# Folding the last query columns of a head with their rotation partners into one tile, and transposing the probabilities two quarters behind their scores

## The chip, the cores and the metric

The kernel runs on one core of one Trainium2 chip. The metric is the device time of one execution in microseconds (us). Engines are named as in the profile: PE is TensorE, PEld its weight loads, DVE is VectorE, ACT is ScalarE, POOL is GpSimd, SP is SyncE.

## The reference, cut to what matters

Four residual steps act on x of 4 x 512 x 512 (batch, sequence, width). In front of each stands a layer norm. The first is a sparse mix along the sequence: for each row of a 512 x 512 similarity the 153 largest entries are kept. The second is a feed-forward layer with a Hadamard rotation and weights quantized to three values, the fourth another one without the rotation. The change lies in the third, a latent attention with 16 heads:

```python
q_hk = (hidden_q @ Wq.T).reshape(Bv, Sv, H, K)
q_big = jnp.einsum('bshk,hkq->bshq', q_hk, w_kc_q)          # 384 query columns per head
q_big = _apply_rope(q_big, sin_q[None, :, None, :], cos_q[None, :, None, :])
q_r = jnp.einsum('bshq,hqr->bhsr', q_big, W_qr)             # 64 columns per head
k_r = jnp.einsum('bld,hdr->bhlr', kv_r, W_kr)
attn = jax.nn.softmax(jnp.einsum('bhsr,bhlr->bhsl', q_r, k_r), axis=-1)
ctx_c = jnp.einsum('bhsl,bld->bhsd', attn, kv_r)
```

`_apply_rope` multiplies each of the 384 columns by its cosine and adds its partner times the sine; the partner of column c is c + 192 or c - 192, with the sign in the sine table.

## The kernel before, in words

Everything of the attention is held transposed, query columns on partitions and the 512 positions along the free dimension, in f32. The loop in `attention` (L798) runs over 32 pairs of heads: 4 batches times 8 groups `g`. While the scores of the current pair are worked on, the queries of the next pair are prepared, in four quarters `j` of 128 positions. A quarter writes `cur.scores(j)`, then a piece of the next pair (`head`, `rope`), then `cur.turn(j - 1)`, the transposes of the quarter before. After the fourth quarter come `nxt.rotated()`, `cur.turn(3)`, `cur.attended()` and `cur.added()`.

- `head(i)` (L674) makes the 128 latent query values `qh` of head i of the pair with four matmuls (L677).
- `rope(i)` (L685) multiplies `qh` by two blocks of `wc` into two PSUM tiles `pb` and rotates them. For i = 0 and 1 these are the first 128 columns of a head and their partners (columns 0 to 127 and 192 to 319, `_query_chunks` L964), with full 128-column matmuls (L693). What is left of a head is 64 columns and 64 partners. In step i = 2 one tile holds the last 64 columns of both heads, the other the partners of both, each written by two 64-column matmuls with `halves` (L661 to L665). VectorE multiplies each tile by the cosine into `ro` (L707) and the other tile by the sine into `rs` (L708); POOL adds the two (L709). `ro` has 7 buffers, `rs` 3.
- `rotated` (L712) multiplies the six `ro` by `wr` into one tile `pr`, the upper 64 rows for one head and the lower 64 for the other: twice `halves` for the first four `ro` (L663, L665), then two full 128-column matmuls (L726) for the last two `ro`, whose block of `wr` has zeros off the diagonal because both heads lie in one tile. ScalarE copies `pr` to `qr` (L731).
- `scores(j)` (L736) has one matmul for each head with 64 rows (L744, L747), VectorE's maximum `nm` (L752), ScalarE's exponential (L755), VectorE's reciprocal (L757) and ScalarE's scaling (L758) of the probabilities `pp`, which have 5 buffers.
- `turn(j)` (L761) transposes the two `pp` of a quarter on TensorE (L766) and copies them to `pT` (L767). `attended` (L769) multiplies `pT` with `kv` into `pc` (L774); `added` (L782) makes `po` (L786) and adds it to x (L791).

The matmul outputs `pqh`, `pb`, `pr`, `pss`, `pc` and `po` share one ring of 4 PSUM tiles. Between the quarters, pieces of background work are written: the top-k search of the next batch (L403, L405) and the feed-forward layers of other batches, each with a planned cost and a due time (L891 to L916). They don't depend on the attention of the same batch. The framework then lays down a fixed order of instructions for each engine, from the order in which they are written, their priorities (`tc.high_priority` for the second of two half-sized matmuls) and its own costs; on the chip each engine runs its order and waits at semaphores. The tags `pp` and `ro` also serve the first and the last stage, when no attention runs (`front_t` L86, `gate_t` L91).

Of the kernel before, what the change touches and what calls it, by code (L numbers as in the profile page):

```python
# [9 lines left out]
F32 = mybir.dt.float32  # L10
# [23 lines left out]
def flamingo_kernel(  # L34
# [51 lines left out]
    def front_t(name):  # L86
        if mine("front", 2):
            return two_k("front", 3, name)
        return wp.tile([P, 512], F32, tag="pp", name=name, bufs=5)
# [30 lines left out]
    cos_q = const.tile([P, 4, S], F32, tag="cosq", name="cos_q")  # L120
    sin_q = const.tile([P, 4, S], F32, tag="sinq", name="sin_q")
# [504 lines left out]
    def hidden_T(b):  # L626
        mv, r = ln_stats([xs[b, j] for j in range(NT)], f"q{b}")
        t = hp.tile([P, NC, S], F32, tag="hT", name=f"hT_{b}", bufs=1)
        for j in range(NT):
            n = wp.tile([P, D], F32, tag="pp", name=f"nq_{b}_{j}", bufs=5)  # L630
# [7 lines left out]
    def query_weights(b, g):  # L638
# [9 lines left out]
        wr = hp.tile([P, 4 * P], F32, tag="wr", name=f"wr_{u}", bufs=1)  # L648
# [18 lines left out]
    class Pair:  # L667
# [17 lines left out]
        def rope(self, i):  # L685
# [3 lines left out]
            for o in range(2):  # L689
                pb = mm_ps(f"pb_{self.u}_{i}_{o}")  # L690
                if i < 2:
                    at = (2 * i + o) * P
                    nc.tensor.matmul(  # L693
                        pb, self.wc[:, at : at + P], self.qhs[i], start=True, stop=True
                    )
                else:
                    at = (4 + o) * P
                    halves(
                        pb, (self.wc[:, at : at + 64], self.wc[:, at + 64 : at + P]), self.qhs,
                        start=True, stop=True,  # L700
                    )
                both.append(pb)
            for o in range(2):
                t = 2 * (i // 2) + o
# [3 lines left out]
                nc.vector.tensor_tensor(rs, both[1 - o], sin_q[:, t, :], ALU.mult)  # L708
# [3 lines left out]
        def rotated(self):  # L712
# [5 lines left out]
            for o in range(2):  # L718
                halves(
                    pr,  # L720
                    (wr[:, 64 * o : 64 * o + 64], wr[:, P + 64 * o : P + 64 * o + 64]),
                    (ros[o], ros[2 + o]),
                    start=(o == 0), stop=False,
                )
            for o in range(2):
                nc.tensor.matmul(  # L726
                    pr, wr[:, (2 + o) * P : (3 + o) * P], ros[4 + o],
                    start=False, stop=(o == 1), skip_group_check=True,
                )
# [6 lines left out]
        def scores(self, j):  # L736
# [12 lines left out]
            for i in range(2):  # L749
# [3 lines left out]
                pp = wp.tile([P, S], F32, tag="pp", name=f"pp_{v}", bufs=5)  # L753
# [44 lines left out]
    def attention(first):  # L798
# [4 lines left out]
        for at, (b, g) in enumerate(order):  # L803
# [3 lines left out]
            for j in range(NT):  # L807
# [13 lines left out]
                if j:  # L821
                    cur.turn(j - 1)
                yield b, g
            if nxt:
                nxt.rotated()
            cur.turn(NT - 1)
# [120 lines left out]
def _constants():  # L947
# [6 lines left out]
    a, a1, c, c1 = _query_chunks()  # L954
# [91 lines left out]
```

## Time and profile before

| What | Time or value |
|---|---|
| median of 3 runs | 2158.28 us (2158.27 to 2160.31) |
| the profiled execution | 2156.5 us |
| its span, first to last instruction | 2154.7 us |
| mean granted TensorE clock | 0.952 |
| 0 to 300 us: first batch's top-k search and feed-forward layer | PE busy 173.3 us, DVE 231.7 us |
| 310 to 1985 us: the 32 pairs | PE idle 96.1 us in all |
| 1985 to 2155 us: the last feed-forward layer | PE busy 140.8 us, DVE 109.5 us |

The page gives busy time for each engine over the whole span, then the span in 40 slices of 53.9 us, each digit a tenth of busy time. A line of the timeline is: start in us, duration in us, engine, line of the code, operation, output from input, the shape of the stationary part for a matmul (rows * columns), output shape from input shape, count; in brackets idle time of the engine in front of it and what ended that. One f32 matmul in the code is two records in the trace. Matmul ends are modelled and overlap the next start, so the distance between starts is the cost.

### The profile page before, as it was taken

What the parts mean: (1) busy time and instruction counts of PE and PEld (TensorE: products, weight loads), DVE (VectorE), ACT (ScalarE), POOL (GpSimd) and SP (SyncE); (2) the same over time, 40 slices, a digit from 0 to 9 for tenths busy, and PEclk for the clock granted to TensorE, in tenths of its full rate; (3) what the DMA queues carried; (4) which work ended last, traced back from release to release, by engine and by line L of the source; (5) the groups of instructions that cost most, each with busy time, mean ns of one, the idle gap of its engine ahead of it and who ended that gap; (6) DMA issues with size and microseconds to landing.
All of it is one profiled execution on the core that took longest, in us unless ns stands there. A gap on an engine that the chain in (4) does not pass through costs nothing.

```text
span 2154.7 us, 21904 instructions
## 1 busy us (share of the span) xinstructions
PE 1901.2 (88%) x7402; PEld 889.7 (41%) x7402; DVE 1571.2 (73%) x3124; ACT 1216.3 (56%) x1991; POOL 347.6 (16%) x332
## 2 busy tenths in 40 slices
PE   1259789999999999899989998999889899999978
PEld 0125534444444434444443334445444344444433
DVE  7986679986676999666669997656637445756765
ACT  6836445445554553466445544565697765567534
POOL 3032012123100121310111222101111110101000
PEclk6579999999999999999999999999999999999989
DMA  7452101111110211111112111111566211111000
GB/s 271 149 182 87 45 27 54 42 47 33 37 32 15 86 49 42 37 37 31 32 28 86 47 44 42 28 29 33 171 217 214 62 37 48 60 37 35 15 15 20
DMA packets 62176, 140.30 MB, mean 65 GB/s; under 512 B 7152, under 2 KB 10608, under 8 KB 58736
## 3 DMA queue, kind: packets, MB, share of 16 engines
q1 hardware_dynamic: 56592, 122.44, 17.9%
q0 software_dynamic: 4320, 14.16, 1.8%
q10 hardware_dynamic: 1152, 2.30, 0.3%
q8 instruction: 59, 0.97, 0.2%
q14 instruction: 53, 0.43, 0.1%
HBM read 118.95 MB, written 19.92 MB: 64 GB/s over the span
## 4 chain that ended last, share of the span: by engine, by line
PE 50%; DVE 34%; ACT 10%; issue 3%; POOL 2%; DMA 1%; SPq 0%; DVEq 0%; POOLq 0%; ACTq 0%
DVE work L405 8%; PE pc L774 7%; DVE m L403 7%; PE po L786 7%; PE pqh L677 5%; DVE nm L752 4%; PE pzh_f L502 3%; PE pss L744 2%; DVE rs L708 2%; PE pu_g L291 2%; PE pd_g L363 2%; PE pd_f L363 2%; PE pg_g L291 2%; PE pu_f L291 2%; PE pb L693 2%
## 5 line engine op out<-in xcount | busy, mean ns | idle before, releaser
L709 POOL TENSOR_TENSOR ro<-ro,rs 128x512 f32<-128x512 f32 x192 | 253.9, 1326 | 1415.8 <-DVE rs L708 1203.1
L755 ACT ACTIVATE pp<-pss,nm 128x512 f32<-128x512 f32 x256 | 175.1, 687 | 257.2 <-DVE nm L752 256.3
L774 PE MATMUL pc<-pT,kv 128*128 128x512 f32 x512 | 244.2, 605 | 14.5 <-ACT pT L767 14.4
L677 PE MATMUL pqh<-hT,wq 128*128 128x512 f32 x512 | 238.6, 606 | 5.0 <-ACT pp L755 3.0
L786 PE MATMUL po<-om,cxo 128*128 128x512 f32 x512 | 231.3, 597 | 1.1 <-ACT cxo L779 1.1
L752 DVE TENSOR_REDUCE nm<-pss 128x1 f32<-128x512 f32 x256 | 169.1, 680 | 78.9 <-PE pss L747 77.5
L403 DVE MAX8 m<-work 128x8 f32<-128x512 f32 x304 | 209.4, 689 | 5.0
L405 DVE MATCH_REPLACE8 work<-m,work 128x512 f32<-128x512 f32 x288 | 194.2, 674 | 0.0
L758 ACT ACTIVATE pp<-pp,rsm 128x512 f32<-128x512 f32 x256 | 179.1, 723 | 25.9 <-DVE rsm L757 25.6
L767 ACT COPY pT<-ppt 128x512 f32<-128x512 f32 x256 | 142.5, 590 | 69.6 <-PE ppt L766 69.6
L766 PEld LDWEIGHTS ppt<-ident,pp 128*128 128x128 f32 x1024 | 119.9, 143 | 95.3 <-issue 46.6
L791 DVE SCALAR_TENSOR_TENSOR x<-po,gt,x 128x512 f32<-128x512 f32 x128 | 95.3, 745 | 86.6 <-PE po L786 85.6
L766 PE MATMUL ppt<-ident,pp 128*128 128x128 f32 x1024 | 148.3, 280 | 10.0 <-ACT pp L758 8.8
L677 PEld LDWEIGHTS pqh<-hT,wq 128*128 128x128 f32 x512 | 93.6, 191 | 132.2 <-issue 93.5
L744 PE MATMUL pss<-kr,qr 64*128 64x512 f32 x256 | 143.4, 641 | 5.1 <-ACT pp L755 4.3
L747 PE MATMUL pss<-kr,qr 64*128 64x512 f32 x256 | 144.6, 645 | 3.4 <-DVE ro L707 3.0
L786 PEld LDWEIGHTS po<-om,cxo 128*128 128x128 f32 x512 | 93.8, 190 | 114.7 <-issue 96.3
L707 DVE TENSOR_TENSOR ro<-pb,cos_q 128x512 f32<-128x512 f32 x192 | 129.8, 676 | 11.1 <-PE pb L693 9.7
L708 DVE TENSOR_TENSOR rs<-pb,sin_q 128x512 f32<-128x512 f32 x192 | 130.1, 678 | 8.9 <-PE pb L693 5.7
L774 PEld LDWEIGHTS pc<-pT,kv 128*128 128x128 f32 x512 | 92.2, 192 | 99.9 <-issue 76.9
L693 PE MATMUL pb<-qh,wc 128*128 128x512 f32 x256 | 126.0, 609 | 6.5 <-ACT qh L682 6.5
L490 DVE TENSOR_TENSOR yb_f<-ya_f 128x1024 f32<-128x1024 f32 x64 | 77.0, 1230 | 15.0 <-PE ph_f L496 14.7
(256 smaller groups left out, 3220.6 us busy)
## 6 DMA issues: line engine op xcount, KB each, us to landing
wq<-in_wqh SPq DMA_DIRECT2D x64, 256.0 KB, 2.6
om<-omd SPq DMA_DIRECT2D x64, 256.0 KB, 2.7
wc<-in_wkcq SPq DMA_DIRECT2D x32, 384.0 KB, 3.0
wr<-in_wqr SPq DMA_DIRECT2D x32, 256.0 KB, 2.6
krd<-krs POOLq DMA_DIRECT2D x32, 256.0 KB, 2.3
kr<-krd SPq DMA_DIRECT2D x32, 256.0 KB, 2.6
sa_w1v<-in_gvT SPq DMA_DIRECT2D x8, 1024.0 KB, 5.3
sb_w1v<-in_gvT SPq DMA_DIRECT2D x8, 1024.0 KB, 6.7
```

Of the source, the lines that this page charges most:

```text
L403: nc.vector.max(m8, cur)
L405: nc.vector.match_replace(work, m8, cur, GONE)
L677: nc.tensor.matmul(pq, self.wqs[i][:, c, :], hT[self.b][:, c, :], start=(c == 0), stop=(c == NC - 1),)
L708: nc.vector.tensor_tensor(rs, both[1 - o], sin_q[:, t, :], ALU.mult)
L709: nc.gpsimd.tensor_tensor(ro, ro, rs, ALU.add)
L744: nc.tensor.matmul(*args, start=True, stop=True)
L752: nc.vector.tensor_reduce(nm, pss[i], AX.X, ALU.max, negate=True)
L755: nc.scalar.activation(pp, pss[i], AF.Exp, bias=nm, accum_out=sm)
L758: nc.scalar.activation(pp, pp, AF.Copy, scale=rs)
L766: nc.tensor.transpose(pt[:, l, :], pp[:, l * P : (l + 1) * P], ident)
L774: nc.tensor.matmul(pc, kv[self.b][:, l, :], self.pT[i][:, l, :], start=(l == 0), stop=(l == NT - 1),)
L786: nc.tensor.matmul(po, self.cxo[i][:, j * P : (j + 1) * P], self.oms[i], start=(i == 0), stop=(i == 1),)
```

## The change

The last step of `rope` is laid out by head instead of by kind. Tile o of step 2 now holds, for head o, its last 64 columns on partitions 0 to 63 and their 64 partners on partitions 64 to 127, made by one full matmul from `qhs[o]`. The cosine multiply is one operation as before. The sine multiply is written as two operations on 64 partitions each, since the partner now lies in the other half of the same tile: partitions 64 to 127 of `pb` go to 0 to 63 of `rs`, and the reverse. In `rotated` the last two `ro` are then multiplied like the others, with one more `halves`, and the zeros in `wr` are gone: `wr` is 192 KB a pair instead of 256, and the cosine and sine tables have 3 blocks of 512 columns instead of 4.

The transposes of a quarter are written two quarters after its scores instead of one: `turn(0)` in quarter 2, `turn(1)` in quarter 3, `turn(2)` and `turn(3)` after `nxt.rotated()`. `pp` has 7 buffers instead of 5, everywhere where the tag is used.

```diff
@@ rope
-                if i < 2:
-                    at = (2 * i + o) * P
-                    nc.tensor.matmul(
-                        pb, self.wc[:, at : at + P], self.qhs[i], start=True, stop=True
-                    )
-                else:
-                    at = (4 + o) * P
-                    halves(
-                        pb, (self.wc[:, at : at + 64], self.wc[:, at + 64 : at + P]), self.qhs,
-                        start=True, stop=True,
-                    )
+                at = (2 * i + o) * P
+                nc.tensor.matmul(
+                    pb, self.wc[:, at : at + P], self.qhs[i if i < 2 else o], start=True, stop=True
+                )
                 both.append(pb)
             for o in range(2):
-                t = 2 * (i // 2) + o
+                t = o if i < 2 else 2
...
                 nc.vector.tensor_tensor(ro, both[o], cos_q[:, t, :], ALU.mult)
-                nc.vector.tensor_tensor(rs, both[1 - o], sin_q[:, t, :], ALU.mult)
+                if i < 2:
+                    nc.vector.tensor_tensor(rs, both[1 - o], sin_q[:, t, :], ALU.mult)
+                else:
+                    for to, fro in ((slice(0, 64), slice(64, P)), (slice(64, P), slice(0, 64))):
+                        nc.vector.tensor_tensor(rs[to, :], both[o][fro, :], sin_q[to, t, :], ALU.mult)
                 nc.gpsimd.tensor_tensor(ro, ro, rs, ALU.add)
@@ rotated
-            for o in range(2):
+            for o in range(3):
+                at = 2 * o * 64
                 halves(
-                    pr,
-                    (wr[:, 64 * o : 64 * o + 64], wr[:, P + 64 * o : P + 64 * o + 64]),
-                    (ros[o], ros[2 + o]),
-                    start=(o == 0), stop=False,
-                )
-            for o in range(2):
-                nc.tensor.matmul(
-                    pr, wr[:, (2 + o) * P : (3 + o) * P], ros[4 + o],
-                    start=False, stop=(o == 1), skip_group_check=True,
+                    pr, (wr[:, at : at + 64], wr[:, at + 64 : at + P]),
+                    (ros[o], ros[2 + o]) if o < 2 else (ros[4], ros[5]),
+                    start=(o == 0), stop=(o == 2),
                 )
@@ scores, hidden_T, front_t
-                pp = wp.tile([P, S], F32, tag="pp", name=f"pp_{v}", bufs=5)
+                pp = wp.tile([P, S], F32, tag="pp", name=f"pp_{v}", bufs=7)
@@ attention
-                if j:
-                    cur.turn(j - 1)
+                if j > 1:
+                    cur.turn(j - 2)
                 yield b, g
             if nxt:
                 nxt.rotated()
+            cur.turn(NT - 2)
             cur.turn(NT - 1)
```

The rest of the diff follows from this: `cos_q` and `sin_q` become `[P, 3, S]`, `wr` becomes `[P, 3 * P]`, and on the host `_constants`, `_pair_columns` and `_pair_rows` put the columns into the new order.

More of the change, by code (lines that the diff above doesn't have):

```diff
@@ L88, in front_t @@
             return two_k("front", 3, name)
-        return wp.tile([P, 512], F32, tag="pp", name=name, bufs=5)
+        return wp.tile([P, 512], F32, tag="pp", name=name, bufs=7)
     def gate_t(name):
@@ L119, in flamingo_kernel @@
     nc.scalar.dma_start(wqk[:, 1, :], wk0T)
-    cos_q = const.tile([P, 4, S], F32, tag="cosq", name="cos_q")
-    sin_q = const.tile([P, 4, S], F32, tag="sinq", name="sin_q")
+    cos_q = const.tile([P, 3, S], F32, tag="cosq", name="cos_q")
+    sin_q = const.tile([P, 3, S], F32, tag="sinq", name="sin_q")
     gx_raw = const.tile([P, 5], F32, tag="graw", name="gx_raw")
@@ L629, in hidden_T @@
         for j in range(NT):
-            n = wp.tile([P, D], F32, tag="pp", name=f"nq_{b}_{j}", bufs=5)
+            n = wp.tile([P, D], F32, tag="pp", name=f"nq_{b}_{j}", bufs=7)
             ln_tile(n, xs[b, j], j, mv, r)
@@ L647, in query_weights @@
         nc.sync.dma_start(wc, wkcq[g])
-        wr = hp.tile([P, 4 * P], F32, tag="wr", name=f"wr_{u}", bufs=1)
+        wr = hp.tile([P, 3 * P], F32, tag="wr", name=f"wr_{u}", bufs=1)
         nc.sync.dma_start(wr, wqr[g])
@@ L953, in _constants @@
     sin = sin * sign
-    a, a1, c, c1 = _query_chunks()
-    order = np.concatenate([a, a1, c, c, c1, c1])
-    q = lambda t: np.ascontiguousarray(t.T[order].reshape(4, P, S).transpose(1, 0, 2))
+    order = np.concatenate(_query_chunks())
+    q = lambda t: np.ascontiguousarray(t.T[order].reshape(3, P, S).transpose(1, 0, 2))
     cosq, sinq = q(cos), q(sin)
@@ L979, in _pair_columns @@
     return np.concatenate(
-        [e[:, :, a], e[:, :, a1], o[:, :, a], o[:, :, a1],
-         e[:, :, c], o[:, :, c], e[:, :, c1], o[:, :, c1]], axis=2
+        [w_[:, :, r] for w_, r in ((e, a), (e, a1), (o, a), (o, a1), (e, c), (e, c1), (o, c), (o, c1))],
+        axis=2,
     )
@@ L990, in _pair_rows @@
     a, a1, c, c1 = _query_chunks()
-    e, o = w[0::2], w[1::2]
-    z = np.zeros((NH // 2, 64, 64), w.dtype)
-    block = lambda r: np.concatenate(
-        [np.concatenate([e[:, r], z], axis=2), np.concatenate([z, o[:, r]], axis=2)], axis=1
-    )
-    return np.concatenate([e[:, a], e[:, a1], o[:, a], o[:, a1], block(c), block(c1)], axis=2)
+    last = np.concatenate([c, c1])
+    return np.concatenate([w_[:, r] for r in (a, a1, last) for w_ in (w[0::2], w[1::2])], axis=2)
 _OUT = ((B, S, D), "float32")
```

## The prediction

> **What bounds the kernel now.** I read the busy line and the 40 slices first, then the busy time by stage, then the timelines of TensorE and VectorE inside one stage, last TensorE's waits.
>
> ```profile
> PE 1901.2 (88%) x7402; PEld 889.7 (41%) x7402; DVE 1571.2 (73%) x3124; ACT 1216.3 (56%) x1991; POOL 347.6 (16%) x332
> ...
> PE   1259789999999999899989998999889899999978
> ...
> DVE  7986679986676999666669997656637445756765
> ```
>
> TensorE looks like the one bound: nine tenths from slice 7 on. But VectorE has three runs of nines (slices 7, 14 to 15, 22 to 24), one for each batch whose top-k search runs behind the attention. Cut at those runs, the busy time by stage (columns: window, its length, then PE, PEld, DVE, ACT, POOL busy with counts, clock, DMA share, GB/s) reads:
>
> ```profile
> 320.00:460.00 140.00, 132.19 (x432) 56.97 (x432) 137.69 (x299) 70.27 (x138) 27.94 (x22) 1.00 0.16 47
> 460.00:700.00 240.00, 230.37 (x992) 114.73 (x990) 165.47 (x288) 124.57 (x224) 38.22 (x36) 0.99 0.11 31
> 700.00:860.00 160.00, 150.31 (x474) 63.18 (x471) 158.29 (x356) 79.81 (x152) 30.55 (x24) 1.00 0.20 60
> 860.00:1140.00 280.00, 262.05 (x1088) 129.53 (x1087) 178.76 (x312) 153.71 (x269) 46.35 (x41) 0.98 0.11 33
> 1140.00:1300.00 160.00, 149.07 (x469) 62.56 (x468) 158.40 (x357) 80.17 (x150) 29.95 (x24) 1.00 0.20 60
> 1300.00:1560.00 260.00, 244.36 (x1018) 119.76 (x1017) 168.26 (x285) 148.39 (x252) 45.79 (x40) 0.97 0.19 59
> 1560.00:1985.00 425.00, 401.29 (x1532) 179.61 (x1531) 244.62 (x498) 298.88 (x455) 62.00 (x48) 0.99 0.28 91
> ```
>
> So there are two regimes. In 140 + 160 + 160 = 460 us VectorE is busy 454.4 us (98.8%) and TensorE 431.6 us (94%): VectorE sets the pace. In the other 1205 us TensorE is busy 1138 us (94%) and VectorE 757 us (63%): TensorE sets it. The 64-column matmuls of `pb`, one per pair of heads, start at 329, 370, 413, 456; 713, 756, 800, 843; 1150, 1193, 1237, 1280 inside the VectorE stretches: 12 pairs there, 19 in the others, and one (at 303 us) in front of the loop.
>
> TensorE's timeline shows what a matmul costs: each f32 one is two records, and the records start 0.43 us apart.
>
> ```profile
> 1020.34 0.64 PE L663 MATMUL pb<-qh,wc 128*64 128x512 f32 x1
> 1020.35 0.64 PE L665 MATMUL pb<-qh,wc 128*64 128x512 f32 x1
> 1020.82 0.59 PE L663 MATMUL pb<-qh,wc 128*64 128x512 f32 x1
> ...
> 1021.68 0.59 PE L663 MATMUL pb<-qh,wc 128*64 128x512 f32 x1
> 1022.21 1.09 PE L766 MATMUL ppt<-ident,pp 128*128 128x128 f32 x8
> ```
>
> L663 and L665 start together: two half-width matmuls take one slot of 2 x 0.43 = 0.86 us. From the last half to the next full-width instruction it is 0.53 instead of 0.43 us: a change of width costs 0.10.
>
> VectorE's timeline gives the price of its operations:
>
> ```profile
> 745.85 0.67 DVE L707 TENSOR_TENSOR ro<-pb,cos_q 128x512 f32<-128x512 f32 x1
> 746.44 0.68 DVE L708 TENSOR_TENSOR rs<-pb,sin_q 128x512 f32<-128x512 f32 x1
> 747.03 0.68 DVE L403 MAX8 m<-work 128x8 f32<-128x512 f32 x1
> ...
> 766.85 0.68 DVE L405 MATCH_REPLACE8 work<-m,work 128x512 f32<-128x512 f32 x1
> 767.56 0.69 DVE L403 MAX8 m<-work 128x8 f32<-128x512 f32 x1
> ```
>
> Independent operations overlap by 0.08 us: start to start is 0.59 us for a duration of 0.67. Where the next must wait for the end (the last two lines) it is 0.71.
>
> [...] No VectorE row here has fewer partitions. [...] The trace has only starts at partition 0, but it has both prices, overlapped 0.59 and waited for 0.71. [...]
>
> **The change, part by part.**
>
> *Projection to pr.* Three slots of half-width matmuls take the place of two such slots and two full ones: minus one slot, 0.86 us a pair. The third `pb` keeps two slots (two full matmuls for two pairs of halves). Where TensorE sets the pace: 19 x 0.86 = -16.3 us. In the 12 other pairs it only adds to TensorE's idle time: nothing.
>
> *Rotation on VectorE.* For the third step of a pair `ro, rs, ro, rs` (4 operations) becomes `ro, rs-half, rs-half, ro, rs-half, rs-half` (6). Two more at 0.59 are 1.19 us: the low bound. [...] 0.71 - 0.59 = 0.12 each, hardly 0.7: with that 1.19 + 0.66 = 1.85 us, the high bound[...]. A gain would need half-tiles to cost half[...]. I take 1.85[...]. In the VectorE stretches nothing hides it: 12 x 1.85 = +22.2 us. In the other 19 it lies in VectorE's idle 37%. In front of the loop nothing else runs: +1.85 - 0.86 = +1.0.
>
> *Transposes two quarters behind.* All counts stay: the same 8 transposes and 2 copies a quarter, one quarter later. What can be had is TensorE's wait for the scaled probabilities, from its waits between 310 and 1980 us (total, times, longest):
>
> ```profile
> PE pc L774 <- ACT pT L767: 14.2, 19, 4.5
> PE pr L663 <- POOL ro L709: 7.9, 9, 1.0
> PE ppt L766 <- ACT pp L758: 7.5, 13, 2.9
> ...
> PE pr L726 <- POOL ro L709: 4.9, 9, 0.9
> ```
>
> Of the 7.5 us only 2.9 (one wait, at 649 us) lie outside the VectorE stretches; the last pair, after 1985, has one of 1.3. I take -3.0, bounds -4.2 and 0. The wait of `pc` for the last copy stays, because the last quarter is still transposed directly before `pc`. What is late next behind the 649 us wait is that same `pc`.
>
> *Order that follows.* In the changed kernel's instruction order 6 of the 128 pairs of score matmuls (L744 with L747), which run side by side now, have transposes between them, so that they take two slots: 0.86 us each, five of them in VectorE stretches (covered by TensorE's 28 us of idle time there), one outside: +0.9. Changes of tile width rise from 376 to 391: 15 x 0.10, two thirds of it outside: +1.0.
>
> *The wait that may grow.* The last step of `pr` now needs both last `ro`: six VectorE operations (4.2 us) and POOL's 1.33 after the first `pb`, where two separate steps needed 2.5 and 3.9 us. Queued behind it on TensorE are the rest of `pc` and `po`, and ScalarE's copy `qr`. The new order puts 4 to 14 us of other TensorE work between in most pairs, 2.8 to 4.7 in about eight. I take +2.0; bounds 0 and 19 x 0.86 = 16.3, which would eat the whole saving.
>
> *At nothing:* `wr` is 192 instead of 256 KB a pair, the two tables are three quarters as long; they land ahead of use, the DMA engines are 11 to 28% busy, and no wait on them stands in the lists. Two more `pp` buffers hold the two more probabilities in flight: the slack of one stays. The POOL adds keep their count, six a pair. SP's queue keeps its order.
>
> Sum: +22.2 - 16.3 + 1.0 - 3.0 + 0.9 + 1.0 + 2.0 = +7.8 us. The profiled execution took 2156.5 us (span 2154.7), so 2164.3 by it; the median of the runs, 2158.3, is 1.8 higher: 2166.
>
> **The rivals.** With *a* us of added VectorE time a pair the sum is 12a - 14.4, so it turns at a = 1.2.
> - *No change.* The half-tiles overlap like all the others, a = 1.19: 12 x 1.19 - 14.4 = -0.1, so 2158. For it: everything on VectorE overlaps in this trace unless it depends on the one before. [...]
> - *Faster.* Half-tiles cost half, two of them one whole, a about 0: VectorE's stretches stay as they are, TensorE keeps its 14.4 us elsewhere: 2144. It decides below a = 0.85. [...] for it: no row here shows a 64-partition operation.
> - *Much slower.* The saved slot doesn't arrive, because the last step of `pr` waits for VectorE and POOL as long as the slot was, in every pair outside: +7.8 + 16.3 = +24, so 2182. For it: `pr` already waits 12.8 us for POOL. Against: the new order moved that step behind other work.
>
> **How the numbers follow.** Forecast 0.45 (its own range 2161 to 2174: a from 1.5 to 2.2, the wait on `pr` from 0 to 6), no change 0.20, faster 0.20, much slower 0.15. A measurement of this kernel tells some 0.2%, 4.3 us, from no change. Faster by more: 0.20 of the faster case and 0.03 of the no-change one, 0.23. Within: 0.14 of no change and 0.06 of the forecast's low end, 0.20. Slower: 0.57. The range 2145 to 2180 leaves out half of the faster and half of the much slower case.
>
> **What would show it.** Right: in the profile after, the 64-partition `rs` rows have about 0.67 us each, x128; from them to the next operation it is near 0.7 us; the pairs in the VectorE stretches take about 45 us where it was 43.3; those elsewhere some 0.8 us less. The matmul row of `pr` at full width is gone. Wrong: half-tiles at 0.3 us, or starts 0.59 apart; pairs outside no shorter, with `pr` waiting more than 5 us longer on POOL in all; or `pc`'s wait for its copies gone, which I hold fixed.

## The result, and the profile after

The changed kernel took 2141.94 us (median of 6 runs, 2138.0 to 2146.4) where the kernel before took 2158.76 (6 runs, 2156.09 to 2160.7): ratio 0.9923 [0.9909, 0.9937], 16.8 us faster. The forecast was 7.8 us slower. The profiled execution took 2146.4 us (span 2144.6), the slowest of the six, so its trace shows 10.1 of the 16.8 us.

The busy line and the slices of the page after:

```profile
PE 1879.9 (88%) x7274; PEld 881.8 (41%) x7274; DVE 1620.3 (76%) x3188; ACT 1211.3 (56%) x1985; POOL 345.8 (16%) x332
...
PE   1259779999998989999989899999889999999878
...
DVE  7986679997766999866669999666735755867675
```

TensorE is 21 us less busy and has 128 records fewer. The missing records are those of `pb`: in the last rotation step two full matmuls take the place of four half-width ones, two matmuls of two records each less, in 32 pairs. `pr` keeps its six matmuls, but they run in three slots of 0.86 us instead of four (the two halves of a slot start 0.01 us apart). VectorE is 49 us busier and has 64 instructions more, two a pair: 1.53 us a pair. Both prices are as forecast in kind; what they did to the time is not. Busy time by stage, the same windows and columns as before:

```profile
320.00:460.00 140.00, 132.11 (x418) 57.21 (x415) 137.29 (x294) 70.66 (x138) 26.65 (x22) 1.00 0.16 47
460.00:700.00 240.00, 226.72 (x977) 113.19 (x977) 175.02 (x305) 125.31 (x226) 39.44 (x37) 0.99 0.10 30
700.00:860.00 160.00, 146.81 (x453) 61.68 (x453) 156.94 (x349) 80.97 (x152) 29.21 (x23) 1.00 0.19 57
860.00:1140.00 280.00, 265.42 (x1089) 129.02 (x1088) 201.97 (x354) 152.30 (x269) 46.36 (x42) 0.98 0.12 33
1140.00:1300.00 160.00, 145.59 (x446) 60.69 (x445) 156.18 (x346) 78.16 (x147) 30.20 (x24) 1.00 0.19 56
1300.00:1560.00 260.00, 240.32 (x1017) 118.98 (x1015) 180.99 (x313) 154.13 (x262) 44.93 (x40) 0.98 0.22 69
1560.00:1985.00 425.00, 406.55 (x1514) 182.96 (x1515) 261.14 (x527) 294.06 (x449) 62.11 (x48) 0.98 0.26 84
```

VectorE still sets the pace in 320 to 460, 700 to 860 and 1140 to 1300 (450.4 of 460 us, 97.9%). Outside, its busy time rose from 757 to 819 us of 1205: 62 us more, where 19 pairs at 1.53 explain 29. So something else is done there that was not done there before. The waits of TensorE between 310 and 1980 us (total, times, longest):

```profile
PE pr L663 <- POOL ro L706: 21.5, 23, 2.9
...
PE ppt L758 <- ACT pT L759: 6.2, 22, 0.5
PE pc L766 <- ACT pT L759: 6.1, 14, 0.7
PE pr L663 <- issue: 5.4, 7, 1.4
...
PE ppt L758 <- ACT pp L750: 2.6, 3, 2.1
```

`pr` waits 8.7 us longer for POOL's last `ro` than the 12.8 of before. `pc` waits 8.1 us less for its copies and `ppt` 4.9 less for the probabilities; 6.2 us are new, transposes that stand back to back and wait for the copy that frees their PSUM tile. The largest of the lines left out are `pb` on `qh`, 9.2 us (6.5 before), and `phT` on the layer norm, 8.9 (7.2 before).

The half-tiles, in the rows of the tile `rs` (shortest, median and longest in ns) and in VectorE's timeline:

```profile
L702 DVE TENSOR_TENSOR rs<-pb,sin_q x128: 656/679/692, 300.4 to 1950.3; 128x512 f32<-128x512 f32 x128
L705 DVE TENSOR_TENSOR rs<-pb,sin_q x128: 683/689/694, 305.3 to 1965.9; 64x512 f32<-64x512 f32 x128
```

```profile
421.50 0.69 DVE L705 TENSOR_TENSOR rs<-pb,sin_q 64x512 f32<-64x512 f32 x1
422.11 0.68 DVE L403 MAX8 m<-work 128x8 f32<-128x512 f32 x1
422.82 0.68 DVE L705 TENSOR_TENSOR rs<-pb,sin_q 64x512 f32<-64x512 f32 x1
423.54 0.09 DVE L405 MATCH_VALUE_LOAD work<-m,work 128x8 f32 x1
```

Half the partitions cost as much as all (689 against 679 ns). MAX8 starts 0.61 us after the first half, overlapping it; the second half starts 0.71 after MAX8, 0.03 behind its end, and the instruction behind it 0.72 later. So these two start late, only when the operation in front has ended, and it costs 0.11 us each (0.71 and 0.72 against 0.61), where 0.12 was taken. A kernel further below (the split alone) shows what goes with it: there the first half reads and writes the same partitions, and it starts 0.61 us after a preceding `ro` (median of 17); in the changed kernel, where it reads partitions 64 to 127 and writes 0 to 63, it starts 0.71 after it (median of 29), and a whole `rs` 0.59 (median of 69).

**Where the 10 us of the trace lie.** I cut each trace where `po` of a pair ends, which gives 32 pairs. Nine of them lie wholly in the VectorE stretches, six at their edges, eight beside a feed-forward layer, eight in the fourth batch, which has no top-k search behind it, and one is the last. A pair is counted here by the queries that are prepared in it: the first pair "of the fourth batch" is the one in which that batch's first queries are made, while the scores of the third batch's last pair are worked on. Durations in us, the forecast's own prices beside them (its +3.9 for order, widths and `pr`'s wait isn't placed):

| Pairs | before | after | measured | forecast |
|---|---|---|---|---|
| 9 in the stretches | 389.1 | 394.0 | +4.9 | +16.7 (9 x 1.85) |
| 6 at their edges | 324.2 | 328.0 | +3.8 | +3.0 (half as the row above, half at -0.86) |
| 8 beside feed-forward work | 533.8 | 511.6 | -22.2 | -6.9 (8 x 0.86), and most of the -3.0 |
| 8 of the fourth batch | 441.4 | 441.6 | +0.2 | -6.9 |
| the last | 79.5 | 83.0 | +3.5 | at most -1.3 |

The first and the third row came out some 12 us lower than forecast each. The fourth and the last came out higher, by 7.1 and about 4.8, and hide a part of that error.

A part of the third row is work that only moved. The order of the changed kernel puts 16 of the feed-forward layer's matmuls (`pd_f`) and some of its transposes (`ptq_hf`) one pair later: beside the feed-forward work there are 144 `pd_f` and 158 `ptq_hf` records instead of 160 and 187, at the edges 32 and 18 instead of 16 and 5, and 16 `ptq_hf` are in the fourth batch. Such a group of 16 `pd_f` takes 3.6 us, so I estimate some 5 us of the 22.2 as moved.

### The profile page after: what moved, and what is told of

The parts are those of the page before. It is cut to its first block, busy times and chain, and to the rows that moved or that the text cites. A ratio compares the mean times of both kernels' runs of the same rounds, so it can differ in the third digit from the quotient of the medians.

```text
span 2144.6 us, 21668 instructions
## 1 busy us (share of the span) xinstructions
PE 1879.9 (88%) x7274; PEld 881.8 (41%) x7274; DVE 1620.3 (76%) x3188; ACT 1211.3 (56%) x1985; POOL 345.8 (16%) x332
## 4 chain that ended last, share of the span: by engine, by line
PE 43%; DVE 40%; ACT 10%; issue 2%; DMA 2%; POOL 1%; ACTq 0%; SPq 0%; POOLq 0%; DVEq 0%
DVE work L405 8%; DVE m L403 8%; PE po L778 6%; PE pc L766 6%; PE pqh L677 5%; DVE nm L744 4%; DVE ro L700 3%; PE pzh_f L502 3%; DVE rs L705 3%; PE pr L663 2%; PE pd_f L363 2%; DVE rs L702 2%; PE pu_g L291 2%; PE pd_g L363 2%; PE pb L692 2%
## 5 line engine op out<-in xcount | busy, mean ns | idle before, releaser
L403 DVE MAX8 m<-work 128x8 f32<-128x512 f32 x304 | 209.4, 689 | 4.5
L692 PE MATMUL pb<-qh,wc 128*128 128x512 f32 x384 | 193.2, 618 | 13.5 <-ACT qh L682 9.2
L758 PE MATMUL ppt<-ident,pp 128*128 128x128 f32 x1024 | 153.6, 284 | 11.1 <-ACT pT L759 7.8
L758 PEld LDWEIGHTS ppt<-ident,pp 128*128 128x128 f32 x1024 | 118.8, 144 | 97.9 <-issue 44.6
L700 DVE TENSOR_TENSOR ro<-pb,cos_q 128x512 f32<-128x512 f32 x192 | 130.5, 680 | 12.6 <-PE pb L692 11.9
L663 PE MATMUL pr<-ro,wr 128*64 128x512 f32 x192 | 98.4, 620 | 28.3 <-POOL ro L706 22.8
L692 PEld LDWEIGHTS pb<-qh,wc 128*128 128x128 f32 x384 | 65.9, 192 | 93.6 <-issue 37.7
```

The costliest lines, as they stand in the source:

```text
L403: nc.vector.max(m8, cur)
L692: nc.tensor.matmul(pb, self.wc[:, at : at + P], self.qhs[i if i < 2 else o], start=True, stop=True)
L700: nc.vector.tensor_tensor(ro, both[o], cos_q[:, t, :], ALU.mult)
L758: nc.tensor.transpose(pt[:, l, :], pp[:, l * P : (l + 1) * P], ident)
```

## The experiments

The change has three parts that can be had singly: the **slot** (last step laid out by head, one TensorE slot less in `pr`), the **split** (two more VectorE operations a pair), and the **turn** (transposes a quarter later, 7 `pp` buffers). Microseconds against the kernel before are the ratio times 2158. The first eight runs take the parts alone and in pairs; edits are shortened.

**Slot and split.** All of the change but the turn (shown against the kernel before).

```diff
-            for o in range(2):
+            for o in range(3):
+                at = 2 * o * 64
...
+                    for to, fro in ((slice(0, 64), slice(64, P)), (slice(64, P), slice(0, 64))):
+                        nc.vector.tensor_tensor(rs[to, :], both[o][fro, :], sin_q[to, t, :], ALU.mult)
```

> The fold alone; transposes one quarter behind and 5 probability buffers, as before. Theory A (the saved slot of pr reaches the end time and the added VectorE operations are pushed out of the saturated stretches into pairs with VectorE time to spare): 2143 to 2149, most of the 17 us gained. Theory B (the transposes' delay gives the gain, the fold is neutral or costs): 2157 to 2166. The step of the prediction that VectorE sets the pace (12 x 1.85 us added): 2169.

Measured: 2153.08 us, 0.9976 [0.9967, 0.9984], -5.2 us. The folding alone is a small gain, not the loss of the forecast, and lies in none of the three ranges expected.

**The turn alone.**

```diff
-                if j:
-                    cur.turn(j - 1)
+                if j > 1:
+                    cur.turn(j - 2)
...
             if nxt:
                 nxt.rotated()
+            cur.turn(NT - 2)
             cur.turn(NT - 1)
```

> The later transposes alone, with 7 probability buffers. To make room, the fourth block of the cosine and sine tables is left out (the last partner columns are multiplied with the third block's values); all operations and shapes stay. Theory A: 2152 to 2158 (only the waits on the scaled probabilities and on the last copies, some 3 us). Theory B: 2140 to 2146, the whole gain.

Measured: 2150.38 us, 0.9962 [0.9948, 0.9976], -8.2 us, between the two ranges expected. The turn is worth nearly three times the 3.0 of the forecast. The run doesn't separate the later transposes from the two more `pp` buffers.

**The split alone**, in the kernel before; input and output stay on the same partitions, and the first half starts 0.61 us after the `ro` in front of it, where it is 0.71 in the changed kernel. VectorE's time hardly differs from the changed kernel's split: the `rs` operations of the nine stretch pairs take 44.4 us here and 44.7 there, 32.0 in the kernel before.

```diff
-                nc.vector.tensor_tensor(rs, both[1 - o], sin_q[:, t, :], ALU.mult)
+                if i < 2:
+                    nc.vector.tensor_tensor(rs, both[1 - o], sin_q[:, t, :], ALU.mult)
+                else:
+                    for h in (slice(0, 64), slice(64, P)):
+                        nc.vector.tensor_tensor(rs[h, :], both[1 - o][h, :], sin_q[h, t, :], ALU.mult)
```

> The kernel before, but the two sine multiplies of the last rope step are written as two 64-partition operations each, on the same partitions: two more VectorE operations a pair, no matmul saved, transposes as before. Theory A: the planner moves top-k work behind, so 2157 to 2163. The prediction's step (nothing hides them in 12 pairs, 1.2 to 1.85 us each): 2173 to 2181.

Measured: 2181.15 us, 1.0109 [1.0095, 1.0123], +23.5 us. That looks like the forecast's +22.2 from VectorE's stretches. It is not, as the table below shows: only +2.8 of it lies there.

**Slot and turn without the split**, from the changed kernel.

```diff
-                    for to, fro in ((slice(0, 64), slice(64, P)), (slice(64, P), slice(0, 64))):
-                        nc.vector.tensor_tensor(rs[to, :], both[o][fro, :], sin_q[to, t, :], ALU.mult)
+                    nc.vector.tensor_tensor(rs, both[o], sin_q[:, t, :], ALU.mult)
```

> The changed kernel with one 128-partition sine multiply in place of the two half ones in the last rope step (it leaves out the exchange with the rotation partner: a column is multiplied with its own value). Takes the added VectorE operations away and keeps everything else. Theory A: 2137 to 2142, at most 5 us below the changed kernel. The prediction's step: 22 us below it, 2120.

Measured: 2134.03 us, 0.9895 [0.988, 0.991], -22.7 us, below the first range expected and well above the second. So the split costs only 6 to 10 us in the changed kernel. TensorE's waits here:

```profile
PE pc L765 <- ACT pT L758: 12.6, 20, 1.8
PE pr L663 <- POOL ro L705: 10.3, 13, 1.2
```

Without the split `pr` waits 10.3 us instead of 21.5. And `pc` waits 12.6 where the changed kernel has 6.1, which suggests that there `pr`'s wait, standing in front of `pc`, covers a part of it.

**The slot alone**, the same edit in the first experiment.

```diff
-                    for to, fro in ((slice(0, 64), slice(64, P)), (slice(64, P), slice(0, 64))):
-                        nc.vector.tensor_tensor(rs[to, :], both[o][fro, :], sin_q[to, t, :], ALU.mult)
+                    nc.vector.tensor_tensor(rs, both[o], sin_q[:, t, :], ALU.mult)
```

> The fold alone (transposes one quarter behind, 5 buffers), with one 128-partition sine multiply in place of the two half ones in the last rope step (leaves out the exchange with the rotation partner). The saved slot of pr without the added VectorE operations and without the later transposes. Theory D (the later transposes are what makes the added VectorE operations cheap, which cost some 20 us without them): 2130 to 2136. Theory E (they cost 6 to 11 us in any order, and the 23 us of the split in the kernel before come from that order): 2140 to 2147.

Measured: 2144.31 us, 0.9944 [0.9929, 0.9958], -12.1 us, somewhat under the forecast's -16.3.

**Turn and split without the slot**: the split's edit in the kernel with the turn alone.

```diff
+                    for h in (slice(0, 64), slice(64, P)):
+                        nc.vector.tensor_tensor(rs[h, :], both[1 - o][h, :], sin_q[h, t, :], ALU.mult)
```

> The later transposes (fourth table block left out, as in the run of them alone), with the sine multiplies of the last rope step split in two on the same partitions. Theory D: the split costs 6 us or less here, 2151 to 2157. Theory E: 6 to 11 us, 2156 to 2162. If the split costs 23 us wherever no matmul is saved: 2173.

Measured: 2171.45 us, 1.0063 [1.0051, 1.0076], +13.6 us.

**The slot given back**: one more full-width matmul in front of each `pr` of the changed kernel.

```diff
             pr = mm_ps(f"pr_{u}")
+            nc.tensor.matmul(pr, wr[:, 0:P], ros[0], start=True, stop=True, skip_group_check=True)
             for o in range(3):
```

> The changed kernel with one more full-width matmul into pr in front of the others, whose result is overwritten: the slot of TensorE is given back in each of the 32 pairs, all else stays. If a slot counts only in the 19 pairs where TensorE sets the pace: 2158, 16 us above the changed kernel. If it counts in all pairs: 2169, 27 us. If the saved slot is worth little and the gain came from the order: under 2150.

Measured: 2167.63 us, 1.0056 [1.0037, 1.0074], +12.1 us, the same as the kernel above that has turn and split but not the slot. The group's row:

```profile
L715 PE MATMUL pr<-ro,wr x64: 592/593/1062, 302.9 to 1984.5; 128*128 128x512 f32 x64
```

Two records a pair, at 0.43 us from start to start 0.86 us, 27.5 us over 32 pairs.

**The changed kernel again**, on the same chip as the three runs above, unchanged.

> The changed kernel once more, beside these on the same chip: 2139 to 2146 by every theory.

Measured: 2144.39 us, 0.9939 [0.9927, 0.9952], -13.2 us. The gain repeats; giving the slot back costs 25.3 us against this run (23.2 by the medians).

What the eight say of each part, in us, each difference uncertain by some 3 to 5 (where two numbers stand, they are with the two measurements of the changed kernel):

| Part | alone | beside the turn | beside slot or split | beside both others |
|---|---|---|---|---|
| split | +23.5 | +21.8 | +6.9 (slot) | +6.1, +9.5 |
| slot | -12.1 | -14.5 | -28.7 (split) | -30.2, -26.8 |
| turn | -8.2 | - | -10.6 (slot), -9.9 (split) | -11.4, -8.0 |

The turn adds to whatever else is there. Slot and split do not: alone the three sum to +3.2, together they give -16.6. The durations of the pairs by kind, from the eight traces, show where:

| Pairs | before | split | turn, split | slot | slot, split | slot, turn | all | slot given back |
|---|---|---|---|---|---|---|---|---|
| 9 in stretches | 389.1 | 391.9 | 390.0 | 385.4 | 393.5 | 382.4 | 394.0 | 391.2 |
| 6 at edges | 324.2 | 332.0 | 331.9 | 327.5 | 324.8 | 327.5 | 328.0 | 330.0 |
| 8 beside feed-forward | 533.8 | 531.7 | 527.4 | 525.7 | 524.1 | 513.0 | 511.6 | 523.6 |
| 8 of batch four | 441.4 | 456.7 | 451.3 | 437.3 | 439.0 | 441.6 | 441.6 | 452.9 |

(The turn alone has 387.5, 323.0, 526.3 and 444.9.) In the nine stretch pairs the split costs 2.8 us alone and 2.5 beside the turn, but 8.1 beside the slot and 11.6 beside both. Slot and turn without it take 6.7 off (389.1 to 382.4), where the forecast had nothing.

The large cost of the split without the slot is +15.3 in batch four and +7.8 at the edges. In its trace two waits are there that the kernel before doesn't have, both at a change of batch; this one falls into the first pair of batch four (TensorE's waits from 1540 to 1985 us):

```profile
PE pt_w1v L228 <- DVE tot_w1v L226: 5.2, 1, 5.2
PE pr L730 <- POOL ro L713: 4.6, 10, 0.8
```

The other is 4.2 us for the similarity matmuls (`psim`, L395). Not all of this is new: the kernel before waits there for the layer norm's transposes (`phT`), 5.5 us in that pair, where the split kernel has 2.5. In the 14 pairs at the edges and in batch four TensorE's idle time rises by 11.1 us in all. Its clock is lower behind such gaps: duration times one minus the granted clock rises from 10.2 to 23.8 us there. Together that is 24.7, about the 23.1 that these pairs became longer.

The same account over all 32 pairs: idle time of TensorE, its clock loss (duration times one minus granted clock), and as work what is left of the duration.

| Kernel | duration | work | idle | clock loss |
|---|---|---|---|---|
| before | 1768.0 | 1643.0 | 101.1 | 23.9 |
| split | 1793.9 | 1641.1 | 115.2 | 37.5 |
| slot | 1757.1 | 1613.3 | 111.4 | 32.4 |
| slot, split | 1764.2 | 1615.7 | 116.1 | 32.4 |
| turn | 1762.7 | 1650.2 | 92.1 | 20.5 |
| turn, split | 1781.5 | 1651.1 | 100.6 | 29.9 |
| slot, turn | 1745.9 | 1621.6 | 100.4 | 23.9 |
| all | 1758.1 | 1623.0 | 109.0 | 26.0 |
| all, again | 1752.8 | 1623.5 | 111.4 | 18.0 |

The slot takes 25 to 30 us of work away in every row, about its 27.5. Alone, 10.3 us of new idle time and 8.5 of clock loss eat most of that; beside the split they don't (+0.9 and -5.1), because that idle time is there already. The split adds no work, only idle time and clock loss: 27.7 us alone, 4.7 beside the slot, 10.7 or 5.1 beside both others. The turn adds 7 to 10 us of work and saves more than that in idle time and clock. So where the parts don't add up, it is in TensorE's waits and its clock, not in its work. In single profiles the clock part is rough, as the last two rows show.

**Is it VectorE being full?** If the split costs because VectorE has no idle time, it should cost nothing once the search is gone from behind the attention. Two kernels leave out all but the first of the 20 rounds of the search there, one the changed kernel, one without the split. (The expectations count 19 rounds; the trace has 320 MAX8 in 16 row blocks, 20 each.)

```diff
             for r in range(rounds):
-                m8 = small.tile([P, 8], F32, tag="m8", name=f"m8_{i}_{r}")
-                nc.vector.max(m8, cur)
...
+                if alone[0] or r == 0:
+                    m8 = small.tile([P, 8], F32, tag="m8", name=f"m8_{i}_{r}")
+                    nc.vector.max(m8, cur)
```

> The changed kernel without 18 of the 19 rounds of the top-k search in the three batches that run behind the attention (it leaves out that part of the search; the plan of the background work and all else stay). VectorE is then not saturated anywhere in the attention. If VectorE's saturation is worth what it seems, the three stretches shorten to what TensorE needs: some 12 pairs at 40 us instead of 43.5, about 2105 us. To be read with the next run.

Measured: 2094.48 us, 0.9712 [0.9697, 0.9726].

```diff
+                if alone[0] or r == 0:
...
-                    for to, fro in ((slice(0, 64), slice(64, P)), (slice(64, P), slice(0, 64))):
+                    nc.vector.tensor_tensor(rs, both[o], sin_q[:, t, :], ALU.mult)
```

> The same without the two added VectorE operations (one whole sine multiply in place of two halves, which leaves out the exchange with the rotation partner). Theory F (the added operations cost because VectorE is saturated in the three stretches): within 3 us of the run before it. Theory G (they cost because the last step of pr waits longer for VectorE and POOL, in any pair): 6 to 10 us below it, as with the top-k search in place.

Measured: 2085.44 us, 0.967 [0.9657, 0.9682]. The split costs 9.0 us with nearly all of the search gone too, so a full VectorE isn't needed for it. The same pair in the kernel before (the expectations of the two tell what each theory wants):

```diff
+                if alone[0] or r == 0:
+                    m8 = small.tile([P, 8], F32, tag="m8", name=f"m8_{i}_{r}")
```

> The kernel before without 18 of the 19 rounds of the top-k search in the three batches behind the attention. If only the order and the clock make the difference between 2158 and the changed kernel's 2142 in the stretches with the search, the fold and the later transposes are worth 16 us here too: 2110. If TensorE sets the pace in all pairs now and the slot counts fully: 2115 to 2120.

Measured: 2111.64 us, 0.9784 [0.9764, 0.9805].

```diff
+                if alone[0] or r == 0:
...
+                    for h in (slice(0, 64), slice(64, P)):
+                        nc.vector.tensor_tensor(rs[h, :], both[1 - o][h, :], sin_q[h, t, :], ALU.mult)
```

> The same with the sine multiplies of the last rope step split in two. With the search in place the split cost 23 us. Theory H (that is 9 us of waits as everywhere, and the rest comes of the crowded VectorE order beside the search): 9 us above the run before it. Theory I (the rest has nothing to do with the search): 20 us or more above it.

Measured: 2138.35 us, 0.9914 [0.9899, 0.9929]. The split costs 26.7 us there. TensorE's waits for the last `ro`, without the split and then with it:

```profile
PE pr L727 <- POOL ro L710: 3.8, 7, 0.9
```

```profile
PE pr L731 <- POOL ro L714: 22.1, 41, 1.2
```

What the split lengthens here is the way from `pb` over VectorE and POOL to `pr`: 18 us more of this wait, with VectorE half idle in the former stretches (busy 49%). The search doesn't explain the interaction of slot and split either: the split costs 26.7 us without the slot and the turn and 9.0 with them.

**Is it the order at the changes of batch?** The layer norm's transposes of the new batch (`hidden_T`) are given priority in three kernels: split alone, slot and turn, slot given back.

```diff
                         if fresh:
-                            hidden_T(nxt.b)
+                            with tc.high_priority():
+                                hidden_T(nxt.b)
```

> The kernel before with the split sine multiplies, and hidden_T (the next batch's transposes) written at high priority, so that the planner puts it on TensorE before the search's first matmul psim and before the sum pt_w1v of the next weights, as in the kernel before. Theory J (13 of the 23 us that the split cost are two stalls at batch boundaries, 4.15 us at psim and 5.2 at pt_w1v with the low clock behind them, because the planner turned the order there): 2165 to 2171. If the boundaries don't matter: 2181.

Measured: 2176.42 us, 1.0085 [1.0071, 1.01]; 5 us better than without the edit (1.0109), by little more than the intervals.

> The changed kernel with one sine multiply (leaves out the exchange with the rotation partner) and hidden_T at high priority. That kernel has the stall at psim at one boundary and not the one at pt_w1v. Theory J: 4 to 7 us less, 2127 to 2130, so that the two added operations cost 12 to 15 us here and not 8. Else: 2134.

Measured: 2138.49 us, 0.9919 [0.9904, 0.9935]; 5 us worse than without (0.9895), again by little more than the intervals.

> The changed kernel with the slot of TensorE given back and hidden_T at high priority. It had both stalls, the changed kernel has neither. Theory J: 10 to 14 us less than without the priority, 2154 to 2158, so that the slot alone is worth 12 to 15 us. Else: 2168.

Measured: 2168.47 us, 1.0047 [1.0032, 1.0063]; without it 1.0056, so no difference that the intervals tell.

The edit took both waits away: `pt_w1v` (5.2 and 5.3 us before) is in none of the three traces, and `psim` waits at most 0.7 us inside the attention, where it had 4.2. But TensorE's wait for the layer norm grew in their place (310 to 1980 us, split alone, where it had 3.4 in all and 2.5 at its longest):

```profile
PE phT L634 <- DVE nq L172: 8.6, 5, 6.8
...
PE psim L395 <- ACT qk L380: 1.3, 2, 0.7
```

The first pair of batch four fell from 64.1 to 58.5 us with the split alone, from 65.8 to 59.5 with the slot given back, and the rest came back in other pairs. Theory J missed in all three, by 5 to 11 us; the third run landed where it was expected without the theory (2168). With both waits gone the split still costs 18 us: taking them away gave some 5 of its 23.

**Three tries at a better kernel**, all slower. ScalarE copies the halves across and POOL multiplies, for both heads:

```diff
-                        nc.vector.tensor_tensor(rs[to, :], both[o][fro, :], sin_q[to, t, :], ALU.mult)
+                        nc.scalar.copy(rs[to, :], both[o][fro, :])
+                    nc.gpsimd.tensor_tensor(rs, rs, sin_q[:, t, :], ALU.mult)
```

> The changed kernel, but in the last rope step ScalarE copies the two halves of each tile across and POOL multiplies them with the sine: VectorE has 2 operations in that step where the changed kernel has 6. ScalarE has four more 0.59 us copies a pair, POOL two more 1.3 us multiplies. If VectorE's time is what counts: 2128 to 2136. If the longer way through ScalarE and POOL to pr counts: 2142 or more.

Measured: 2272.48 us, 1.0537 [1.0522, 1.0552].

```profile
PE pr L663 <- POOL ro L707: 72.8, 28, 4.6
PE ppt L759 <- ACT pT L760: 22.9, 22, 2.9
```

The way to `pr` became longer still, and ScalarE's copies of `pT` queue behind the new ones.

For one head only:

```diff
+                        if o:
+                            nc.vector.tensor_tensor(rs[to, :], both[o][fro, :], sin_q[to, t, :], ALU.mult)
+                        else:
+                            nc.scalar.copy(rs[to, :], both[o][fro, :])
+                    if o == 0:
+                        nc.gpsimd.tensor_tensor(rs, rs, sin_q[:, t, :], ALU.mult)
```

> The same for the first of the two heads only: VectorE has 4 operations in the last rope step, as many as the kernel before. If VectorE's time is what counts: 2132 to 2138, near the run with one sine multiply (2134). If the way to pr counts: 2142 or more.

Measured: 2171.34 us, 1.0068 [1.0051, 1.0084]; `pr` waits 25.4 us for POOL, `ppt` 13.8 for the copies.

The folded step a quarter earlier, so that `pr` ends on a step without halves:

```diff
                     elif j == 2:
-                        nxt.rope(1)
-                    else:
                         nxt.rope(2)
+                    else:
+                        nxt.rope(1)
```

> The changed kernel with its last two rope steps exchanged: the folded step, with its six VectorE operations, runs in the third quarter, and the step of the second head, with four, in the fourth; pr takes the folded columns first. All counts stay. Theory G (the added operations cost by the wait of pr for the last ro): most of the 7 us between the changed kernel and the one with a single sine multiply comes back, 2132 to 2138, and TensorE's idle time in front of pr falls from 27 to about 15 us. If the place of the six operations doesn't matter: 2140 to 2145.

Measured: 2196.93 us, 1.0183 [1.0165, 1.0201], a miss.

```profile
PE pb L692 <- DVE rs L705: 32.6, 30, 2.3
PE pr L663 <- POOL ro L706: 15.3, 22, 1.2
```

`pr`'s wait on POOL fell from 21.5 to 15.3 us, but now the next step's `pb` waits for the PSUM tile that the half-tiles still read: 32.6 us that weren't there. No version that computes everything was faster than the changed kernel.

## Why the prediction was wrong, step by step

**Prices: right.** Half-tile 0.69 us (0.67 to 0.68 was taken), a late start 0.11 (0.12), the slot 0.86. That half-tiles take as long as whole ones, and that six starts a pair are late, were my assumptions: no operation of VectorE in the trace of before has fewer than 128 partitions. VectorE's added busy time is 1.53 us a pair instead of 1.85, inside its bounds: not all six are late, as MAX8 above, between the halves, starts 0.61 us after the first.

**"In the VectorE stretches nothing hides it: 12 x 1.85 = +22.2 us": the step that failed.** It takes the work in a stretch as given. In the nine full pairs I summed VectorE's time from start to start, without idle time: the `rs` operations rose from 31.9 to 45.3 us, 13.4 or 1.49 a pair, close to the price. The nine pairs got 4.9 us longer, where 16.7 was forecast. But the top-k operations there fell from 219.4 to 213.8, the residual adds, the adjacency tile and the layer norms' small operations by about 5 together, and idle time rose by 2. The rounds of the search (MAX8 of L403, VectorE's busy time and count in the window), in the kernel before:

```profile
320.00:460.00 140.00, 43.61 (x64) 1.00 0.16 47
...
700.00:860.00 160.00, 49.34 (x72) 1.00 0.20 60
860.00:1140.00 280.00, 3.44 (x5) 0.98 0.11 33
1140.00:1300.00 160.00, 50.58 (x74) 1.00 0.20 60
```

and in the changed kernel:

```profile
320.00:460.00 140.00, 40.58 (x60) 1.00 0.16 47
...
700.00:860.00 160.00, 46.53 (x68) 1.00 0.19 57
860.00:1140.00 280.00, 11.06 (x16) 0.98 0.12 33
1140.00:1300.00 160.00, 46.59 (x68) 1.00 0.19 56
```

In the three stretches 14 rounds fewer are done, and 11 more in 860 to 1140 alone, where VectorE is busy 72% of the time. The windows are fixed in time, and the stretches of the changed kernel end up to 6 us later, so part of this is only a longer search; cut at the ends of pairs it is 4 rounds of 168 in the nine full pairs (the 5.6 us above, with their replacements), done in the edge pairs instead. The search isn't tied to a pair, and the framework's fixed order places it anew. This could be read in the changed kernel's order of instructions before any run: from one pair's last `nm` to the next pair's, the nine pairs hold 349 search operations in the order of before and 331 in the changed one, and the pair behind the first stretch 4 and then 11. I had read that order for TensorE's steps and not for the search. The experiments divide the 4.9: beside slot and turn the split does cost 11.6 us in these pairs, most of its 13.4 of VectorE time, and slot and turn take 6.7 off: with them alone VectorE is busy 376.3 us in the nine pairs, 381.2 before and 383.9 in the changed kernel. So the stretch isn't free, but its work isn't fixed under any of the three edits either. It isn't the whole cost: with nearly all of the search gone the split still costs 9.0 us.

**The slot, "19 x 0.86 = -16.3", and nothing in the 12 others: right in size, and in place but for one pair.** Given alone, the slot gains 12.1 us: 8.1 in the eight feed-forward pairs (6.9 forecast), 4.1 in batch four (6.9), 3.7 in the nine stretch pairs, and 3.3 lost at the edges. In the changed kernel batch four as a whole gains nothing, since its first pair is longer, before and after:

```profile
1558.30:1613.10 54.80, 47.68 (x161) 22.51 (x160) 21.55 (x48) 52.54 (x65) 7.64 (x6) 0.94 0.63 220
```

```profile
1546.40:1608.00 61.60, 50.22 (x172) 24.03 (x172) 23.58 (x51) 57.87 (x70) 7.61 (x6) 0.89 0.65 217
```

It has 61.6 us instead of 54.8, at a clock of 0.89; its longest waits are 7.0 us for `phT`, where it was 5.5, and a new one of 2.1 for `pr`. The seven behind it take 380.0 instead of 386.6, 0.94 less each in the mean, near the slot; singly they range from 6.9 less to 3.3 more. Giving the slot back costs 12.0 us beside the feed-forward work and 11.3 in batch four, 1.4 to 1.5 a pair where the matmul takes 0.86. Beside the feed-forward work the 16 `pd_f` and some transposes come back with it, some 5 us of the 12.0; in batch four TensorE's work rises by only 5.8, and 3.8 of idle time and 1.7 of clock come with it.

**The transposes, "-3.0": under-sized.** Measured -8.2 alone, -8.0 to -11.4 in the other three places. "The wait of `pc` for the last copy stays" was wrong: 14.2 to 6.1 us in the changed kernel, 14.2 to 9.1 with the turn alone. That the last quarter is still transposed in front of `pc` was true, but the quarter before it now stands there as well, and its copies and transposes fill the time, as far as the lists of waits tell. The second part was not in the sum at all. In the feed-forward pairs a short wait is followed by a low clock. TensorE's timeline of the kernel before (the bracket is idle time in front, and what ended it):

```profile
1390.63 1.12 PE L744 MATMUL pss<-kr,qr 64*128 64x512 f32 x2
1393.27 2.07 PE L747 MATMUL pss<-kr,qr 64*128 64x512 f32 x2 [1.52 <-DVE ro L707]
1395.27 1.11 PE L663 MATMUL pb<-qh,wc 128*64 128x512 f32 x1
```

and the granted clock around it (third column from the end of each window):

```profile
1390.00:1395.00 5.00, 3.48 (x11) 1.25 (x9) 5.00 (x9) 4.34 (x8) 2.30 (x2) 0.81 0.00 0
1395.00:1400.00 5.00, 5.00 (x15) 1.89 (x15) 4.05 (x5) 0.11 (x1) 1.17 (x1) 0.50 0.24 56
```

The second matmul of a score pair, meant to run beside the first (at 1009 us it starts 0.01 us behind it), waits 1.52 us for a PSUM tile that VectorE still reads; then the clock is 0.50 over the next window. At 954 us there is another such wait of 1.52 us, and the clock is 0.50 for 3.41 us from 956.2 us on. The two pairs as a whole (70.1 and 71.7 us), and the same two in the changed kernel:

```profile
921.10:991.20 70.10, 67.82 (x283) 32.62 (x282) 42.58 (x64) 43.72 (x69) 8.54 (x6) 0.98 0.09 29
1360.00:1431.70 71.70, 69.42 (x282) 32.96 (x284) 42.56 (x64) 43.72 (x69) 8.54 (x6) 0.95 0.10 28
```

```profile
925.40:992.20 66.80, 64.58 (x279) 31.38 (x279) 43.14 (x65) 41.28 (x67) 8.53 (x6) 1.00 0.10 29
1356.70:1423.40 66.70, 64.48 (x278) 31.30 (x278) 43.04 (x65) 41.29 (x67) 8.53 (x6) 1.00 0.10 29
```

TensorE is as idle as before (2.2 us in each), but at full clock, and 3.2 and 4.9 us less busy. Over the eight feed-forward pairs the 22 us come from 11.2 of work (6.9 the slot, some 5 moved to other pairs), 6.8 of clock and 4.2 of idle time. With the turn alone the clock loss there falls from 11.9 to 6.8, with slot and turn to 3.4; with the slot alone it stays at 11.9.

**"The wait that may grow", +2.0: under-sized.** It grew by 8.7 us, 12.1 with the part that the trace puts down to issue (2.0 to 5.4). I had named more than 5 us as a sign of a wrong step if the outer pairs got no shorter. They did get shorter: 5.7 of the 9.2 us that all idle time in front of `pr` rose by, from pair to pair, lie in the nine stretch pairs (8.0 to 13.7), where TensorE isn't what sets the pace.

**The others.** "In front of the loop +1.0" is too small to be told. Split scores (+0.9) and changes of width (+1.0) can't be told apart, but by the account of all 32 pairs the turn adds 7 to 10 us to TensorE's work, so this term was too small. The last pair, at which only a gain was seen, is 3.5 us longer; 2.5 of it is TensorE's idle time and 1.7 lower clock.

**The rivals.** "Faster" had the time nearly right (2144) and the cause wrong: half-tiles don't cost half (689 ns against 679), and the stretches did not stay as they were. "Much slower" had the right mechanism for what the split costs in the changed kernel, the wait of `pr`, at half of its size (8.7 against 16.3 us).

**What stays open.** Why the split costs 22 to 27 us where the slot isn't saved and 6 to 10 where it is. The difference lies in TensorE's waits and clock loss; why these rise so unequally isn't shown. Shown: it isn't the search, and it isn't the two waits at the changes of batch, whose removal gave 5 us in one kernel and none that can be told in another. Every edit also gives the framework another order, and no run holds the order fixed. The lost clock varies between runs of the same kernel (26.0 and 18.0 us over the 32 pairs of the two profiles of the changed kernel), which limits what single profiles can tell here.

## What to carry to other kernels

A stretch in which one engine is full has two kinds of work, tied and movable: price an addition there only after reading, in the changed order, how much movable work stays in it. The same holds for the cut by kind of pair: count what moved across it before a row is put down to a cause. Where slots and waits are near balance, the parts of a change don't add up, so measure them together as well as alone; a single part that hits its forecast (the split, +23.5 against +22.2) can do so for another reason. Two waits of 1.52 us on a busy TensorE were followed here by 1.7 and 3.4 us of lost clock, more than the waits themselves, so a change that removes a few short waits can be worth more than their sum.

## What the hardware showed that was not expected

- Gaps of only 1.52 us were followed by a granted clock of 0.50: at 1393 us in the next 5 us window, at 954 us from 1.8 us behind the gap on. It isn't always so: of the 28 gaps of 1.3 us or more between 315 and 1985 us in the two profiles, before and after, 18 were followed by the low clock, which began in the gap or at most 3.1 us behind it, and why the others weren't is not shown. The low clock came in pieces of 3.41 us or a multiple (there 14 of 3.41, four of 6.83 and one of 10.24 us), and each 3.41 us of it lost 1.7. The run with the longest idle time (ScalarE's copies, 195 us over the pairs) also lost most to the clock, 90 us against 24 in the kernel before.
- A half-tile operation on 64 partitions took 689 ns and one on 128 partitions 679. A half that reads partitions 64 to 127 and writes 0 to 63 starts 0.71 us after a preceding `ro`, where one that reads and writes the same partitions (the split alone) starts 0.61 after it.
